# First stage of a four-layer graph kernel: sorted rows fetched early, loads and buffers rearranged

## Chip, cores, metric

One core of one Trainium2 chip. The time is the device time of one execution in microseconds (us). A kernel's executions agree within half a per cent. Each ratio is taken against the kernel before in the same rounds (its median was 2303.0 to 2304.5 in all of them). The changed kernel was timed in other rounds than the experiments, so differences from its median carry 1 to 2 us of noise. A difference from before is called a gain or a loss where the 95% interval of the ratio leaves out 1.

## The reference, cut

Four graph layers, each with a residual and a layernorm. Only the first, over a hypergraph, is concerned. B = 8 batches, N = 2048 nodes, E = 64 hyperedges, F = 64 features; H says which node belongs to which hyperedge (one certain and about 2 more per node).

```python
h = x @ W
s = leaky_relu(h @ a_node, 0.2)
alpha = softmax(where(H.T > 0, s[:, None, :], NEG), axis=-1)
agg = einsum('ben,bnf->bef', alpha, h)                       # hyperedge features
beta = sigmoid((h @ a_gn)[:, None, :] + (agg @ a_ge)[:, :, None])
all_he = elu(beta[..., None] * h[:, None] + (1 - beta[..., None]) * agg[:, :, None])
coefs1 = softmax(where(H[None] > 0, (tanh(elu(agg) @ fcW + fcb) @ av)[:, None, :], NEG), -1)
g = einsum('bne,benf->bnf', coefs1, all_he)                  # per node, over its hyperedges
industry = einsum('nm,bmf->bnf', adj / deg, x @ W_ind)       # 2048 x 2048 product
# ... attention over (industry, g), layernorm, three more layers that use adj
```

## The kernel before

The nodes are sorted by their number of hyperedges, so that a tile of 128 sorted nodes needs as many *slots* as its fullest node: 12 for tile 0, then 5, 5, 4, 4, 4, 3, ... , 1; 57 in all. The first stage has these parts:

- **x tiles** (16): h by TensorE, exponentials by ScalarE, three multiplies by VectorE, a write of the hidden rows to `hs_hbm`.
- **Adjacency load**: 32 halves of 512 KB through 4 staging buffers; ScalarE casts each into a tile that stays.
- **Tables** tab2, ts2 of the hyperedges, from the sums over all x tiles.
- **Sorted rows**: 16 gathers of H (hs), transposes, and a running count that gives `slot`.
- **Blocks**: per tile a gather `hrow` of sorted hidden rows; per slot three matmuls into a PSUM tile pz, then VectorE, ScalarE, VectorE, VectorE and GpSimd.
- **Filler**: 576 matmuls of the adjacency products (64 `du` for the degrees, 512 `u`), which a generator gives out between the slots to keep TensorE busy.

```python
for t in range(NT):                       # in the x stage's pool "pa"
    xt[t] = pa.tile([P, NP, P], F32, tag="xt", bufs=4)
    eng = nc.sync if t % 2 == 0 else nc.scalar
    eng.dma_start(xt[t], x_t[t])
# ... order, 16 x tiles, tables ...
for t in range(NT):                       # adjacency; staging also in "pa"
    for k in range(2):
        a = pa.tile([P, HN], F32, tag="a", bufs=4)
        eng = nc.sync if k == 0 else nc.scalar
        eng.dma_start(a, adj_t[t * P:(t + 1) * P, cols(k, HN)])
        nc.scalar.copy(adj[t][:, cols(k, HN)], a)
# ---- "pa" ends; pool "pb" takes its memory
filler = products()                       # du, then u; one matmul per next()
# ... hs: 16 gathers of h_ne by order; m2, pt, mt, pcm -> slot ...
def begin(t):
    # hrow <- gather of hs_hbm; split into hrh (ScalarE), hrl (VectorE);
    # o: one-hot per slot (GpSimd); ps = o @ ts2; R, rs, co (VectorE)
now = begin(0)
for t in range(NT):
    S, both, ohs, R, co = now
    for s in range(S):
        # pz = ident @ hrh + ident @ hrl + o[s] @ tab2
        if s == 0 and t + 1 < NT:
            fill(3)
            now = begin(t + 1)
        fill(10)
        # VectorE: z = pz * R; ScalarE: y = exp(z - 1); VectorE: y = min(max(z, 1), y)
        # VectorE: y * co; GpSimd: acc += y
```

Instructions of one engine run in the order that the build chose. The matmuls of blocks and filler keep the order of the program; everything else a scheduler orders, so the place of a loop in the program is a priority, not a time.

## Time and profile before

| | us |
|---|---|
| before, median of the 3 runs known at the prediction (spread) | 2305.34 (2302.71 to 2307.01) |
| first hrow gather, "the gate" | 131.68 |
| first pz * R multiply | 143.17 |
| next stage's first instruction | 343.14 |

How to read it: the kernel has 2301 us of trace, of which the first stage is 343. Most profile lines of before stand in the prediction. Here are, in addition, two of the waits of SyncE's queue and one of ScalarE (who waited, for what: us in total, times, longest), and the long stretch in one row of the view by stretches (bounds, length, busy TensorE, its weight loads, VectorE, ScalarE, GpSimd, granted clock, DMA share, GB/s):

```profile
SPq L364 <- DVE st L356: 25.5, 8, 7.7
SPq L238 <- PE ph L337: 21.7, 5, 5.6
```
```profile
ACT adj L437 <- DMA a<-in_adj_t: 26.5, 11, 6.3
```
```profile
143.20:330.40 187.20, 187.20 (x827) 152.44 (x827) 153.29 (x288) 51.73 (x88) 93.99 (x96) 0.97 0.23 70
```

The new queues are to cure the waits of the first fence. In the long stretch TensorE is busy for all of 187.2 us, and VectorE for 153.3.

### The profile page before, as it was taken

To read this page: it belongs to the slowest core of one execution; us is meant where nothing else is said; L and a number is where in the kernel's file an instruction comes from. 1 tells how busy PE (TensorE), PEld (TensorE's weight loads), DVE (VectorE), ACT (ScalarE), POOL (GpSimd) and SP (SyncE) were. 2 spreads that over 40 slices of the span, in tenths; PEclk is the share of its full clock that TensorE was granted. 3 is DMA by queue.
4 is the path that set the end of the run, shared out by engine and by line. 5 is a ranking of instruction groups with operands and counts; after the bars stand their busy time and mean duration, and the time that the engine had idled before them with its cause. 6 is when DMAs were issued, how large, how long until landed. Compare 5 with 4: busy or idle time off the path is not lost.

```text
span 2301.2 us, 19853 instructions
## 1 busy us (share of the span) xinstructions
PE 2009.9 (87%) x7382; PEld 1293.3 (56%) x7382; DVE 1119.7 (49%) x1895; ACT 361.7 (16%) x610; POOL 468.2 (20%) x432
## 2 busy tenths in 40 slices
PE   5379977887993999979999999999996999899994
PEld 3258863335882444447447446546543777777873
DVE  4347983554544122222882784685585334341322
ACT  2412323331111111101001001000000011111110
POOL 0155524550332332310010010011001001020202
PEclk8779998999995999989999999999998999999997
DMA  7712223220000000010000000000000223210000
GB/s 245 233 38 63 84 95 91 69 60 1 1 1 12 0 19 19 19 41 1 9 8 3 7 7 5 5 10 5 5 7 11 73 70 82 72 30 1 19 1 20
DMA packets 92586, 88.64 MB, mean 39 GB/s; under 512 B 62976, under 2 KB 63232, under 8 KB 92416
## 3 DMA queue, kind: packets, MB, share of 16 engines
q1 hardware_dynamic: 65072, 61.35, 9.3%
q10 hardware_dynamic: 23568, 16.95, 2.5%
q0 software_dynamic: 3840, 8.98, 1.5%
q8 instruction: 60, 0.98, 0.2%
q14 instruction: 46, 0.38, 0.1%
HBM read 66.22 MB, written 21.04 MB: 38 GB/s over the span
## 4 chain that ended last, share of the span: by engine, by line
PE 47%; DMA 8%; DVE 7%; POOL 3%; issue 2%; ACT 1%; SPq 0%; DVEq 0%; ACTq 0%; POOLq 0%
PE py L826 17%; PE u L773 10%; PE u L459 9%; PE u L171 8%; DMA a<-in_adj_t 7%; DVE a L932 2%; POOL ln_r L155 1%; PE pr L171 1%; PE tr L137 1%; DVE xg L115 1%; POOL r L838 1%; DVE ln_c L145 1%; DVE ln_v L151 1%; ACT r L149 0%; PE s L764 0%
## 5 line engine op out<-in xcount | busy, mean ns | idle before, releaser
L826 PE MATMUL py<-wp,xg 128*128 128x512 f32 x1024 | 448.6, 597 | 8.4 <-DVE pr L831 5.7
L826 PEld LDWEIGHTS py<-wp,xg 128*128 128x128 f32 x1024 | 193.6, 191 | 254.4 <-issue 216.3
L459 PE MATMUL u<-adj,vh 128*128 128x512 f32 x768 | 236.2, 410 | 24.7 <-ACT vh L166 20.9
L171 PE MATMUL u<-adj,hi 128*128 128x512 f32 x768 | 255.2, 413 | 0.0
L171 PE MATMUL u<-adj,lo 128*128 128x512 f32 x768 | 246.1, 400 | 1.0 <-DVE lo L897 1.0
L773 PE MATMUL u<-pt,xn 128*128 128x512 f32 x512 | 228.3, 604 | 8.3 <-DVE u L782 7.1
L459 PE MATMUL u<-adj,vl 128*128 128x512 f32 x768 | 228.9, 402 | 0.0
L831 DVE TENSOR_TENSOR pr<-py,emb_n 128x512 f32<-128x512 f32 x256 | 177.0, 691 | 51.9 <-PE py L826 37.4
L832 DVE TENSOR_REDUCE r<-pr 128x32 f32<-128x512 f32 x256 | 175.5, 685 | 8.1
L459 PEld LDWEIGHTS u<-adj,vh 128*128 128x128 f32 x768 | 141.8, 190 | 64.2 <-ACT vh L166 22.7
L773 PEld LDWEIGHTS u<-pt,xn 128*128 128x128 f32 x512 | 97.6, 193 | 130.6 <-issue 116.1
L171 PEld LDWEIGHTS u<-adj,hi 128*128 128x128 f32 x768 | 142.8, 190 | 41.0 <-issue 11.8
L171 PEld LDWEIGHTS u<-adj,lo 128*128 128x128 f32 x768 | 144.1, 189 | 34.5 <-DVE lo L897 1.4
L459 PEld LDWEIGHTS u<-adj,vl 128*128 128x128 f32 x768 | 141.4, 190 | 31.4 <-issue 0.7
L834 POOL TENSOR_TENSOR r<-r,bias 128x256 f32<-128x256 f32 x32 | 23.4, 730 | 636.4 <-DVE r L832 636.4
L155 POOL TENSOR_TENSOR ln_r<-ln_e,neg_half 128x8 f32<-128x8 f32 x64 | 105.7, 1651 | 185.5 <-DVE ln_e L153 185.2
L767 DVE TENSOR_SCALAR pt<-pt 128x512 f32<-128x512 f32 x64 | 48.8, 780 | 173.6 <-ACT pt L766 172.1
L771 POOL TENSOR_TENSOR acc<-acc,pt 128x512 f32<-128x512 f32 x60 | 79.6, 1327 | 163.3 <-DVE pt L767 160.5
L916 POOL TENSOR_TENSOR r<-r,xn 128x512 f32<-128x512 f32 x16 | 20.5, 1278 | 420.9 <-DVE r L915 420.9
L932 DVE SCALAR_TENSOR_TENSOR a<-a,adj 128x512 f32<-128x512 f32 x64 | 44.6, 697 | 124.7 <-DMA a<-in_adj_t 124.4
L156 DVE TENSOR_TENSOR xn<-ln_c,ln_r 128x512 f32<-128x512 f32 x48 | 41.8, 871 | 92.2 <-POOL ln_r L155 92.2
L655 POOL DMA_INDIRECT gn<-gs_hbm,rank x64 | 67.8, 1060 | 81.1 <-PE tr L137 62.3
(292 smaller groups left out, 2418.7 us busy)
## 6 DMA issues: line engine op xcount, KB each, us to landing
a<-in_adj_t SPq DMA_DIRECT2D x64, 256.0 KB, 2.8
a<-in_adj_t SPq DMA_DIRECT2D x16, 512.0 KB, 6.7
a<-in_adj_t ACTq DMA_DIRECT2D x16, 512.0 KB, 6.8
gs_hbm<-acc SPq DMA_DIRECT2D x16, 256.0 KB, 2.0
u_hbm<-ut SPq DMA_DIRECT2D x16, 256.0 KB, 2.8
ut<-u_hbm SPq DMA_DIRECT2D x16, 256.0 KB, 3.1
u_hbm<-u SPq DMA_DIRECT2D x16, 256.0 KB, 2.3
xg<-u_hbm SPq DMA_DIRECT2D x32, 128.0 KB, 2.7
```

The costliest lines, as they stand in the source:

```text
L155: nc.gpsimd.tensor_tensor(rstd, vare, neg_half[:, :groups], ALU.pow)
L156: nc.vector.tensor_tensor(dst, xc, rstd[:, :, None].to_broadcast([P, groups, F]), ALU.mult)
L171: tc.keep_in_program_order(nc.tensor.matmul(*args, **kw))
L459: nc.tensor.matmul(u[c], lhsT=half[:, j, :], rhs=adj[t][:, cols(c)], start=t == 0 and i == 0, stop=ends and not own,)
L655: nc.gpsimd.indirect_dma_start(out=gn[:, j, :], out_offset=None, in_=g_rows, in_offset=bass.IndirectOffsetOnAxis(ap=rank4[:, p, c * JT + j ...
L767: nc.vector.tensor_scalar(pt, pt, 1.0, None, op0=ALU.max)
L771: nc.gpsimd.tensor_tensor(acc, acc, pt, ALU.add)
L773: nc.tensor.matmul(u[p], lhsT=xn[:, p, t, :], rhs=pt, start=t == 0, stop=t == NT - 1)
L826: nc.tensor.matmul(py.rearrange("p o d -> p (o d)"), lhsT=xg[b][:, q, cols(j, P)], rhs=wp[:, q, cols(k)], start=q == 0, stop=q == 1,)
L831: nc.vector.tensor_tensor(pr, py, e_b, ALU.mult)
L832: nc.vector.tensor_reduce(r[:, j, b, cols(k, OH)], pr, AX.X, ALU.add)
L932: nc.vector.scalar_tensor_tensor(a, a, 1.0, adj[t][:, cols(k)].bitcast(F32), op0=ALU.mult, op1=ALU.not_equal, accum_out=left[:, t, k:k + 1],)
```

## The change

Its intent: do the sorted rows beside the loads rather than after them, so that the blocks begin earlier, and make room and queues for it. Cut to its core:

```diff
+    slot = hy.tile([P, N], BF16, name="slot")            # outer pool: live through the stage
+    hs = hy.tile([P, NT, E], F32, name="hs")
-            xt[t] = pa.tile(..., bufs=4)
-            eng = nc.sync if t % 2 == 0 else nc.scalar
-            eng.dma_start(xt[t], x_t[t])
+            xt[t] = pa.tile(..., bufs=6)
+            nc.scalar.dma_start(xt[t], x_t[t])
+        for t in range(NT):                               # adjacency loop, now ahead of the x tiles,
+            for k in range(2):                            # staging in a pool "ad" of its own
+                a = ad.tile([P, HN], F32, tag="a", name="a", bufs=4)
+                eng = nc.sync if k == 0 or t < NT // 2 else nc.scalar
+                eng.dma_start(a, adj_t[t * P:(t + 1) * P, cols(k, HN)])
+                nc.scalar.copy(adj[t][:, cols(k, HN)], a)
...
-            eng = nc.sync if t % 2 == 0 else nc.scalar
-            eng.dma_start(hs_hbm[t * P:(t + 1) * P, :], st)
+            nc.scalar.dma_start(hs_hbm[t * P:(t + 1) * P, :], st)
...   (the hs gathers, m2, pt, mt, pcm and slot move from the pool "pb" to behind the x tiles)
-            for c in range(NCH):                          # x for the products: 4 buffers -> 3,
-                fetch(0, c)                               # fetched and split within the du loop
+            for c in range(3):
+                fetch(0, c)
...
-                o = pl.tile([P, P], F32R, tag="o", name="o", bufs=17)
+                o = pl.tile([P, P], F32R, tag="o", name="o", bufs=13)
...
-                if s == 0 and t + 1 < NT:
-                    fill(3)
+                if s == max(0, S - 5) and t + 1 < NT:
+                    fill(3 if t else 0)
                     now = begin(t + 1)
-                fill(10)
+                fill(12 if t else 0)                      # no filler in tile 0, 12 per slot later
```

More of the change, by code (lines that the diff above doesn't have):

```diff
@@ L207, in tile_gnn_fast @@
     adj = [adj_pool.tile([P, N], F32R, name=f"adj{t}") for t in range(NT)]
-    with tc.tile_pool(name="pa", bufs=1) as pa, tc.tile_pool(name="pa_ps", bufs=1, space=PSUM) as pps:
+    with tc.tile_pool(name="ad", bufs=1, side="right") as ad, tc.tile_pool(
+        name="pa", bufs=1
+    ) as pa, tc.tile_pool(name="pa_ps", bufs=1, space=PSUM) as pps:
         m_n = pa.tile([P, NT, E], F32, name="m_n")
@@ L235, in tile_gnn_fast @@
         for t in range(NT):
-            xt[t] = pa.tile([P, NP, P], F32, tag="xt", name=f"xt{t}", bufs=4)
-            eng = nc.sync if t % 2 == 0 else nc.scalar
-            eng.dma_start(xt[t], x_t[t])
+            xt[t] = pa.tile([P, NP, P], F32, tag="xt", name=f"xt{t}", bufs=6)
+            nc.scalar.dma_start(xt[t], x_t[t])
+        HN = N // 2
+        for t in range(NT):
[4 more added lines that the diff above has]
+                nc.scalar.copy(adj[t][:, cols(k, HN)], a)
         pw = pps.tile([P, 2], F32, tag="sm", name="pw", bufs=2)
@@ L372, in tile_gnn_fast @@
         )
+        for t in range(NT):
+            nc.gpsimd.indirect_dma_start(
+                out=hs[:, t, :], out_offset=None, in_=h_ne,
+                in_offset=bass.IndirectOffsetOnAxis(ap=order[:, t:t + 1], axis=0),
+            )
+        for c in range(NCH):
+            m2 = pa.tile([P, JT, 2, E], F32, tag="m2", name="m2", bufs=2)
+            for i in range(2):
+                nc.vector.tensor_scalar(m2[:, :, i, :], hs[:, c * JT:(c + 1) * JT, :], 0.0, None, op0=ALU.is_gt)
+            pt = pps.tile([P, C], F32, tag="sm", name="pt", bufs=2)
+            for j in range(JT):
+                nc.tensor.transpose(pt[:, cols(j, P)], m2[:, j].rearrange("p i e -> p (i e)"), ident)
+            mt = pa.tile([P, C], BF16, tag="mt", name="mt", bufs=2)
+            nc.scalar.copy(mt, pt)
+            pcm = pps.tile([P, C], F32, tag="sm", name="pcm", bufs=2)
+            nc.tensor.matmul(pcm, lhsT=tri2, rhs=mt, start=True, stop=True)
+            nc.vector.tensor_tensor(slot[:, cols(c)], pcm, mt, ALU.mult)
         gv = pagg[:, :, 0:G * (F + 1)].rearrange("p k (g c) -> p k g c", c=F + 1)
@@ L428, in tile_gnn_fast @@
         nc.vector.tensor_tensor(ts2[E:P, :], tsf, ts2[0:E, :], ALU.subtract)
-        HN = N // 2
-        for t in range(NT):
-            for k in range(2):
-                a = pa.tile([P, HN], F32, tag="a", name="a", bufs=4)
-                eng = nc.sync if k == 0 else nc.scalar
-                eng.dma_start(a, adj_t[t * P:(t + 1) * P, cols(k, HN)])
-                nc.scalar.copy(adj[t][:, cols(k, HN)], a)
     def load_x(dst, p, c):
@@ L472, in tile_gnn_fast @@
     with ExitStack() as pb_scope:
-        pb = pb_scope.enter_context(tc.tile_pool(name="pb", bufs=1))
+        pb = pb_scope.enter_context(tc.tile_pool(name="pb", bufs=1, side="right"))
         pps = pb_scope.enter_context(tc.tile_pool(name="pb_ps", bufs=1, space=PSUM))
@@ L482, in fetch @@
             def fetch(p, c):
-                xc[p, c] = pb.tile([P, JT, P], F32, tag="x", name="xc", bufs=4)
+                xc[p, c] = pb.tile([P, JT, P], F32, tag="x", name="xc", bufs=3)
                 load_x(xc[p, c], p, c)
@@ L489, in parts @@
                 part[c] = split(pb, xc.pop((p, c)), f"v{c}", 1, [P, JT, P])
-            for c in range(NCH):
+            for c in range(3):
                 fetch(0, c)
             for t in range(NT):
+                if t in (2, 3, 4):
+                    parts(0, t - 2)
+                    if t == 2:
+                        fetch(0, 3)
+                if t == 8:
+                    parts(0, 3)
                 for c in range(NCH):
@@ L496, in products @@
                     yield
-            for c in range(NCH):
-                parts(0, c)
             for c in range(NCH):
@@ L514, in products @@
                         if p + 1 < NP and t % JT == JT - 1:
-                            if g == 0:
+                            if g == 0 and t // JT < 3:
                                 fetch(p + 1, t // JT)
-                            else:
+                            elif g == 1:
                                 parts(p + 1, t // JT)
+                                if t // JT == 0:
+                                    fetch(p + 1, 3)
                         if p == 0 and g == 0 and t == 3:
@@ L547, in fill @@
                 next(filler, None)
-        slot = pb.tile([P, N], BF16, name="slot")
-        with tc.tile_pool(name="pc", bufs=1) as pc:
-            hs = pc.tile([P, NT, E], F32, name="hs")
-            for t in range(NT):
-                nc.gpsimd.indirect_dma_start(
-                    out=hs[:, t, :], out_offset=None, in_=h_ne,
-                    in_offset=bass.IndirectOffsetOnAxis(ap=order[:, t:t + 1], axis=0),
-                )
-            for c in range(NCH):
-                m2 = pc.tile([P, JT, 2, E], F32, tag="m2", name="m2", bufs=2)
-                for i in range(2):
-                    nc.vector.tensor_scalar(m2[:, :, i, :], hs[:, c * JT:(c + 1) * JT, :], 0.0, None, op0=ALU.is_gt)
-                pt = pps.tile([P, C], F32, tag="mm", name="pt", bufs=3)
-                for j in range(JT):
-                    transpose(pt[:, cols(j, P)], m2[:, j].rearrange("p i e -> p (i e)"))
-                mt = pc.tile([P, C], BF16, tag="mt", name="mt", bufs=2)
-                nc.scalar.copy(mt, pt)
-                pcm = pps.tile([P, C], F32, tag="mm", name="pcm", bufs=3)
-                mm(pcm, lhsT=tri2, rhs=mt, start=True, stop=True)
-                nc.vector.tensor_tensor(slot[:, cols(c)], pcm, mt, ALU.mult)
         pl = pb_scope.enter_context(tc.tile_pool(name="pl", bufs=1))
```

## The prediction

> **What bounds the kernel now.** I began with the chain of waits. It covers only 719.9 to 2301.2 us, stages that the diff does not touch, so it says nothing about the first stage. I therefore read that stage in stretches: busy us of each engine, granted clock, share of the 16 DMA engines, GB/s.
>
> ```profile
> 10.00:20.00 10.00, 5.41 (x31) 4.20 (x28) 6.43 (x33) 3.65 (x7) 0.00 (x0) 0.98 0.94 338
> ...
> 70.00:80.00 10.00, 5.86 (x30) 3.67 (x31) 6.31 (x18) 5.11 (x12) 0.00 (x0) 1.00 0.88 279
> ...
> 90.00:105.00 15.00, 2.71 (x18) 1.86 (x16) 0.66 (x4) 8.22 (x12) 0.00 (x0) 0.50 0.59 187
> 105.00:131.60 26.60, 6.78 (x20) 3.40 (x20) 7.16 (x16) 5.10 (x9) 15.33 (x16) 0.50 0.43 100
> 131.60:142.90 11.30, 6.18 (x15) 4.48 (x16) 2.35 (x7) 0.62 (x1) 10.12 (x18) 0.50 0.17 47
> 142.90:165.10 22.20, 22.20 (x87) 18.05 (x86) 13.81 (x25) 5.10 (x9) 11.69 (x14) 0.86 0.09 25
> ...
> 260.00:300.00 40.00, 40.00 (x180) 32.48 (x179) 37.14 (x69) 11.33 (x19) 19.26 (x20) 1.00 0.21 70
> ...
> 330.40:343.10 12.70, 2.66 (x11) 1.54 (x10) 10.16 (x21) 2.39 (x4) 2.52 (x2) 0.76 0.28 104
> ```
>
> The first number after the comma is TensorE. Up to 105 us the transfers bound the stage (0.6 to 0.94 of the DMA engines); from 105 to 142.9 TensorE does 13 us of work in 38; from 142.9 to 330.4 it is never idle; the last 12.7 us belong to VectorE. The timeline and the waits name the edges:
>
> ```profile
> 78.81 0.68 DVE L360 TENSOR_TENSOR ex<-ph,ex 128x512 f32<-128x512 f32 x1
> ...
> 94.55 0.17 DVE L428 TENSOR_TENSOR ts<-tsm,ts 64x16 fp32r<-64x16 f32 x1 [1.05 <-ACT ts L427]
> ...
> 131.68 0.94 POOL L575 DMA_INDIRECT hrow<-hs_hbm,order  x1 [5.56 <-DVE slot L568]
> ...
> 142.93 1.05 PE L171 MATMUL du<-adj,ones_r 128*128 128x512 f32 x2
> 143.17 0.70 DVE L616 TENSOR_TENSOR pz<-pz,R 128x512 f32<-128x512 f32 x1 [0.61 <-PE pz L171]
> ...
> 343.14 0.17 DVE L120 MEMSET bd_ind<- 128x128 f32 x1 [2.47 <-DMA gs_hbm<-acc]
> ```
> ```profile
> POOL hs L553 <- ACT adj L437: 103.4, 1, 103.4
> ```
>
> The last of the 16 x tiles is done at 79.5; the hyperedge tables at 94.7; the gathers of sorted rows (hs) begin only when the last adjacency cast has freed memory, near 105.4; their transposes and slot tables end at 131.4; the first block's gather follows at 131.7, its first multiply at 143.2; the next stage starts at 343.1.
>
> **What the Trainium skill says.** "DMA: Bandwidth & Descriptors", section "Issuing engines are not separate DMA queues": transfers from different engines end up on the same 16 DMA engines, and several issuers save only issue time. The trace agrees: a 512 KB adjacency half lands in 6.7 us from SyncE and 6.8 from ScalarE. So "x on its own queue" buys no bandwidth, only freedom from blocking. The same page, "Anatomy of one DMA", says that any wait for a semaphore happens on the issuing sequencer before dispatch. The trace agrees: SyncE's queue waits 25.5 us in total for VectorE's st and 21.7 us for TensorE's ph, with adjacency loads queued behind. The other side: a transfer issued by ScalarE holds up ScalarE's arithmetic. "TensorE: Matmul & The Clock Gate", "What's actually happening": the idle default is half clock, and sustained work releases it. The trace agrees: 0.50 from 90 to 142.9, 1.00 later.
>
> **The change part by part.**
>
> 1. Removed: the stretch from 105.4 to 131.7, 26.3 us of gathers, transposes and slot tables. The same 16 gathers, 16 transposes and 4 slot multiplies now lie beside the loads.
>
> 2. Moved: the gate. In the built program the first hrow gather waits for the last hs_hbm write and for the last VectorE instruction of the first pool (ts2), because the block pool reuses its memory. It no longer waits for an adjacency cast directly. So everything hangs on when the x tiles end, 79.5 in the old kernel.
>
> 3. The x tiles get later. In the built order ScalarE casts 5 adjacency halves, then tiles 0 and 1, 6 more casts, tiles 2 and 3, further casts up to the 17th, tile 4, casts up to the 29th, tile 5; tiles 6 to 15 come only after the 32nd cast. VectorE's tiles 2 and 3 also stand behind the compares of gathered rows. Estimates from the old durations: the order table is ready near 23 (25.9 before; two x tiles' vector work of 3 us moves behind it, about 1 us is lost to later small loads). Gathers go out every 1.25 us and land in some 3 us; the eighth lands near 37 and holds ScalarE at cast 11 for about 6 us, the twelfth near 42 holds it about 4 us more. By cast 17, about 50 us. The other 15 halves are 7.9 MB; at 280 to 310 GB/s that is 25 to 28 us, so the casts end near 78. Total bytes to then: 16.8 MB adjacency, 3.4 x, 0.5 + 0.5 H, 1.3 hs writes = 22.5 MB; at the 320 to 340 GB/s of the full stretches that alone is 68 us after a start at 7, which agrees. Tiles 6 to 15 then need TensorE's 1.09 + 1.17 us each, with little slack: about 2.35 us x 10 = 23.5. The last tile ends near **101.5**, 22 us later than now.
>
> 4. The tables take 15.2 us now (79.5 to 94.7); without adjacency casts between them on ScalarE about 12. The gate opens near 113.5, against 131.7: **18 us earned**. The setup of a first block stays 11.3 to 11.5 us.
>
> 5. Tile 0 has 12 slots and no filler now. The first du matmul stands behind the 13th pz, and pz has 3 buffers, so it waits for about 10 slots on VectorE: 10 x 3 x 0.69 = 20.7, plus tile 1's small operations and split, 1.3 + 0.7, plus leading pz multiplies: **about 24 us** in which TensorE has only 3 matmuls per slot. In the old kernel du began with the first slot. So du begins at 113.5 + 11.5 + 24 = 149, against 142.9: 6 us *later*.
>
> 6. Given back: of the 57 slots the old stretch from du to the last filler holds 53 (one before it, three after), the new one 44 (13 before it), so it loses 9 x 3 = 27 pz matmuls: 27 x 0.2325 (two in 0.465 at full clock) = 6.3 us. 188 becomes 181.5. The filler (12 per slot) now lasts to the last slot, so the tail from last filler matmul to the next stage shrinks from 12.7 to about 5.5 (two ut multiplies 1.3, a write 2.8, the last slot's chain).
>
> Sum: 149 + 181.5 + 5.5 = 336 against 343.1: **7 us saved**, all else unchanged. 2305.3 - 7 = **2298 us**. Of the 26 us removed most is lost to the later x tiles (22), and the rest to tile 0 without filler; what remains comes from the balance of the tail.
>
> **The rivals.**
>
> A. The whole stretch is earned. If the x tiles kept their 79.5, the gate would open near 92, and the sum gives 29 us saved, 2276 us. For it: the diff means it so, and x has six buffers and its own queue. Against it: ScalarE's order, ten tiles behind the last cast.
>
> B. The load becomes the bound. The adjacency now has at most four halves in flight, mostly from one queue, and ScalarE stalls twice in front of casts. At 230 GB/s, which the old stretch 40 to 50 shows, 22.5 MB takes 98 us and the casts end near 105; the x tiles end near 128 and the kernel loses about 20 us: 2325. Against it: 338 GB/s where nothing blocked, 10 to 20 us.
>
> C. VectorE becomes the bound in the long stretch. It is at 37.1 of 40 us from 260 to 300. But there it is beside 10 filler per slot; 12 filler leave 45 slots' multiplies for the same filler. I estimate 142 us of VectorE in 181. Then nothing changes there; if its order nevertheless holds TensorE, a few us are lost, near 2302.
>
> D. Later stages shift by layout or clock: I see no mechanism, and allow 3 us.
>
> **Range and chances.** The x tiles' end is uncertain by about 7 us, tile 0 by 3, tail and later stages by 3 each: together some 9 us, so 8 in 10 lie within about 13: 2284 to 2311. Two per cent is 46 us. Even rival A saves less; the whole idle time before du is what would be needed. Faster 0.02, same 0.965, slower 0.015.
>
> **What would show it right or wrong.** The last ex multiply of the x tiles near 101 (79.5 before), with casts ended near 78 and x tiles alone after them. The first hrow gather near 113, released by ts2. Twelve pz triples with no du among them and VectorE near full for 24 us. The first du near 149, TensorE never idle from there for about 181 us, and the last filler within 6 us of the next stage, which begins near 336. It is wrong if the x tiles end before 90 (rival A) or after 110 (B), if du begins before 135, or if TensorE shows gaps in the long stretch (C).

## The result, and the profile after

| | before (with a fourth run) | after |
|---|---|---|
| median, us (runs) | 2304.53 (4) | 2305.65 (4) |
| spread | 2302.71 to 2307.01 | 2302.95 to 2309.39 |
| profiled execution, clock | 2301.2, 0.944 | 2302.0, 0.943 |

The ratio is 1.0005 with a 95% interval of 0.9986 to 1.0024: no difference. Ratios here are the mean time of one kernel's fast runs over that of the other's of the same rounds, so not quite the ratio of the medians quoted.

The first stage in the changed kernel, by stretches (columns as above):

```profile
20.00:50.00 30.00, 16.54 (x67) 10.62 (x67) 10.88 (x38) 15.13 (x23) 15.43 (x16) 0.60 0.90 317
50.00:88.00 38.00, 6.24 (x24) 4.04 (x25) 3.78 (x12) 16.24 (x21) 0.00 (x0) 0.64 0.66 228
88.00:111.30 23.30, 21.31 (x112) 13.65 (x112) 18.27 (x52) 5.17 (x23) 0.00 (x0) 0.93 0.39 137
111.30:123.10 11.80, 5.75 (x28) 3.94 (x28) 5.43 (x14) 3.12 (x8) 0.03 (x1) 0.70 0.06 23
```
```profile
134.60:161.90 27.30, 16.77 (x42) 10.31 (x42) 26.26 (x41) 8.13 (x14) 18.83 (x22) 0.63 0.11 29
161.90:338.00 176.10, 176.03 (x797) 144.12 (x795) 136.13 (x268) 46.75 (x79) 80.05 (x78) 0.99 0.26 79
338.00:341.70 3.70, 0.00 (x0) 0.00 (x0) 2.36 (x5) 0.00 (x0) 0.00 (x0) 0.94 0.71 263
```

To 50 us the transfers run at 317 GB/s. Then for 38 us everything is slow: DMA engines at 0.66, ScalarE busy 16 of 38, VectorE nearly idle. Only at 88 do the remaining ten x tiles run, at TensorE's pace (21.31 of 23.30 us). Tile 0 (second fence) has VectorE at 26.3 of 27.3 us and TensorE at 16.8, at a granted clock of 0.63; from 161.9 TensorE is never idle. The timeline names the edges (start, length, engine, line, operation, idle time before it and what ended that):

```profile
49.74 0.49 ACTq L248 DMA_DIRECT2D a<-in_adj_t  x1
49.77 1.04 ACT L249 CAST adj<-a 128x1024 fp32r<-128x1024 f32 x1
50.28 0.49 ACTq L248 DMA_DIRECT2D a<-in_adj_t  x1
...
57.77 1.99 ACT L249 CAST adj<-a 128x1024 fp32r<-128x1024 f32 x2 [6.59 <-DMA a<-in_adj_t]
...
110.50 0.68 DVE L371 TENSOR_TENSOR ex<-ph,ex 128x512 f32<-128x512 f32 x1
...
123.07 0.94 POOL L580 DMA_INDIRECT hrow<-hs_hbm,order  x1 [79.34 <-DVE ts L457]
...
134.58 0.70 DVE L622 TENSOR_TENSOR pz<-pz,R 128x512 f32<-128x512 f32 x1 [0.53 <-PE pz L171]
...
161.89 1.48 PE L171 MATMUL du<-adj,ones_r 128*128 128x512 f32 x3
...
341.66 0.17 DVE L120 MEMSET bd_ind<- 128x128 f32 x1 [1.31 <-DMA u_hbm<-ut]
```

ScalarE issues two adjacency halves at 49.74 and 50.28; the next cast in its stream needs one of them, and begins 7.5 us later. This occurs four times (with idle times of 6.6, 3.9 in two pieces, 4.4 and 5.5 us), since eight of the halves are ScalarE's. The gate opens at 123.07, released by ts2, 8.6 us earlier than before; but the stretch from the first multiply (134.58) to the next stage (341.66) is 207.1 us, 7.1 longer than before. The two cancel to 1.5 us. Of that, little reaches the next stage's own first gather (343.72 before, 343.44 after), and the rest of the kernel is as it was within the spread of the runs.

So the question is twofold: why the gate opens no earlier, and why the stretch behind it got longer.

### The profile page after: what moved, and what is told of

Read it like the earlier page. It is cut to its first block, busy times and chain, and to the rows that moved or that the text cites. A ratio compares the mean times of both kernels' runs of the same rounds, so it can differ in the third digit from the quotient of the medians.

```text
span 2302.0 us, 19820 instructions
## 1 busy us (share of the span) xinstructions
PE 2010.0 (87%) x7382; PEld 1295.4 (56%) x7382; DVE 1118.9 (49%) x1895; ACT 363.1 (16%) x610; POOL 470.0 (20%) x432
## 4 chain that ended last, share of the span: by engine, by line
PE 47%; DMA 8%; DVE 7%; POOL 3%; issue 2%; ACT 1%; SPq 0%; DVEq 0%; ACTq 0%; POOLq 0%
PE py L832 17%; PE u L779 10%; PE u L479 9%; PE u L171 8%; DMA a<-in_adj_t 7%; DVE a L938 2%; POOL ln_r L155 1%; PE pr L171 1%; PE tr L137 1%; DVE xg L115 1%; POOL r L844 1%; DVE ln_c L145 1%; DVE ln_v L151 1%; ACT r L149 0%; PE s L770 0%
## 5 line engine op out<-in xcount | busy, mean ns | idle before, releaser
L171 PEld LDWEIGHTS u<-adj,hi 128*128 128x128 f32 x768 | 143.6, 191 | 40.9 <-issue 11.5
```

Of the source, the lines that this page charges most:

```text
L171: tc.keep_in_program_order(nc.tensor.matmul(*args, **kw))
```

## The experiments

Theory: (a) the halves that ScalarE issues itself lay their landing time bare and hold everything behind the casts; (b) without filler in tile 0 TensorE stands idle there, and its work is done later. Rivals: the transfers are at their rate anyway; VectorE's chain sets the length of the stretch whatever the filler does. Twelve kernels ran, all gave correct results. Edits are against the changed kernel unless "before" is said. The table at the end of this section collects gates and stretches.

**1. All adjacency loads on SyncE.**

```diff
-                eng = nc.sync if k == 0 or t < NT // 2 else nc.scalar
+                eng = nc.sync
```

> The changed kernel with all 32 adjacency halves issued by SyncE (the changed kernel gives 8 of them to ScalarE). Theory 1: those halves stand in ScalarE's own stream just before the casts that need them, so their landing time of 6.5 to 8 us is laid bare four times; then the casts end near 78 instead of 88, the first block gather opens near 113.5 instead of 123.1, and the kernel takes about 2296 us, 9 less than the changed one. Rival 2: the transfers are at their rate anyway, or the other waits (sorted rows, buffers) hold the casts: the casts end within 2 us of 88 and the time stays within 3 us of 2305.

Measured: 2290.85 us, ratio to before 0.9939 (0.9925 to 0.9952). The casts end at 79.2, the last x tile at 96.4, the gate opens at 108.3:

```profile
108.29 0.95 POOL L580 DMA_INDIRECT hrow<-hs_hbm,order  x1 [66.16 <-DVE ts L457]
```

ScalarE's waits for adjacency transfers up to 90 us, first in the changed kernel, then here, and the stretch 60 to 80 of both in the same order:

```profile
ACT adj L249 <- DMA a<-in_adj_t: 26.3, 14, 6.6
```
```profile
ACT adj L249 <- DMA a<-in_adj_t: 13.2, 17, 1.7
```
```profile
60.00:80.00 20.00, 0.00 (x0) 0.00 (x0) 0.48 (x2) 9.93 (x12) 0.00 (x0) 0.50 0.77 261
```
```profile
60.00:80.00 20.00, 9.90 (x42) 6.47 (x39) 6.75 (x19) 13.30 (x21) 0.00 (x0) 0.79 0.90 347
```

The longest wait falls from 6.6 to 1.7 us, and in the same 20 us 347 instead of 261 GB/s move, x tiles now among them. Theory (a) holds for the casts, which end 8.8 us earlier. The gate gains more than expected, 14.8 us, for a reason that the edit does not show: the build put ScalarE's work in another order too. Behind the last cast come seven x tiles here and ten in the changed kernel, so the last one ends 17.2 us after the casts and not 23.2. These 6.0 us and the 8.8 make up the 14.8; no run separates them. Of the 14.8 us 12.7 reach the next stage (341.66 to 328.97), since the stretch is 2.1 us longer.

**2. Filler in tile 0 as everywhere.**

```diff
-                    fill(3 if t else 0)
+                    fill(3)
-                fill(12 if t else 0)
+                fill(12)
```

> The changed kernel with filler matmuls in tile 0 as in all other tiles (12 per slot, 3 before the next block). Theory 1: TensorE's work from the gate on is fixed (about 747 matmuls of 0.2325 us) and tile 0 without filler leaves about 11 us of it undone; then du begins near 136 instead of 161.9, the next stage near 331 instead of 341.7, and the kernel takes about 2294 us. Rival 2: VectorE carries tile 0, and filler before its pz only delays it, so what TensorE gains at the start VectorE lacks at the end: 2300 to 2306 us, with the tail from last filler to next stage over 10 us.

Measured: 2305.4 us, 1.0007 (0.9993 to 1.002): nothing. Theory (b) in this form fell. du begins at 135.8 and TensorE is full up to 313, and there the filler is used up:

```profile
300.00:313.00 13.00, 13.00 (x59) 10.65 (x58) 9.11 (x19) 3.00 (x5) 5.75 (x6) 1.00 0.14 44
313.00:340.00 27.00, 17.12 (x46) 10.50 (x44) 26.83 (x58) 7.90 (x14) 9.62 (x9) 0.61 0.27 88
```

Before 313 TensorE is full and VectorE is at 0.70; after it VectorE is full (26.83 of 27.00) and TensorE is not. The stretch with VectorE as the bound has only moved from the start to the end.

**3. x tiles first: the adjacency loop told after the tables**, as in the kernel before, the rest of the change kept.

```diff
-        (adjacency loop ahead of pw, rank and x tiles)
         nc.vector.tensor_tensor(ts2[E:P, :], tsf, ts2[0:E, :], ALU.subtract)
+        (adjacency loop, same text, still with staging in "ad")
```

> The changed kernel with the adjacency loop told to the scheduler after the hyperedge tables, as in the kernel before, all else of the change kept (staging memory of its own, sorted rows early, x on ScalarE's queue, no filler in tile 0). Theory 1: only the order on ScalarE made the x tiles late; then the last x tile ends near 78, the first block gather goes out near 92 to 95 (before: 131.7, changed: 123.1), du begins near 132, the next stage near 312, and the kernel takes about 2272 us. Rival 2: x tiles and loads share ScalarE's queue, and the loads of x that now wait there for buffers push casts and tiles alike: the gate stays after 115 and the time over 2295 us.

Measured: 2288.49 us, 0.9932 (0.9919 to 0.9946). The last x tile ends at 83.9 and the gate opens at 100.25, but the first multiply comes only at 119.83, where SyncE alone had brought it too. Timeline:

```profile
100.25 0.94 POOL L581 DMA_INDIRECT hrow<-hs_hbm,order  x1 [51.78 <-DVE ts L449]
...
114.16 2.94 ACT L457 CAST adj<-a 128x1024 fp32r<-128x1024 f32 x3 [3.86 <-DMA a<-in_adj_t]
...
117.85 0.79 PE L171 MATMUL pz<-hrh,ident_r 128*128 128x512 f32 x1 [9.17 <-ACT hrh L166]
```

The order did keep the x tiles late, as theory 1 says; but a new wait took the place of the old. The block's own cast hrh stands behind the last adjacency casts in ScalarE's stream, and the last three wait for a half that ScalarE issued. Half of the expected gain came.

**4. The kernel before with the 64 du matmuls ahead of the sorted rows.**

```diff
+        fill(64)
         slot = pb.tile([P, N], BF16, name="slot")
```

> The kernel before with one line added: the 64 du matmuls are given out ahead of the gathers of sorted rows, so that they run in the stretch 105 to 132 in which TensorE idles. Nothing else of the change. Theory 1: the end of the stage is set by TensorE's work left when the long stretch begins; 64 x 0.2325 = 14.9 us of it leave, the next stage begins near 330 instead of 343 and the kernel takes about 2291 us. Rival 2: VectorE (37 of 40 us busy from 260 to 300) takes over as the bound, or the slot tables come later because their transposes stand behind du: 2300 to 2310 us.

Measured: 2302.56 us, 0.9991 (0.9977 to 1.0005): nothing. du ran early, from 95.1 on, and TensorE had 15 us less to do, but with 10 filler per slot the last filler matmul came at 312 rather than 330, and from there to 341.9 VectorE carried the stage alone, busy for 25.96 of the last 29.2 us. The gate also opened 3.6 us later (135.3). So both parts of rival 2 came, the first by the same mechanism as in run 2.

**5. The kernel before with one part of the change: sorted rows early** (hs and slot in the outer pool, gathers and count behind the x tiles; nothing else).

```diff
+    slot = hy.tile([P, N], BF16, name="slot")
+    hs = hy.tile([P, NT, E], F32, name="hs")
+        (hs gathers, m2, pt, mt, pcm, slot behind the x tiles, as in the change)
-        (the same in pool "pc" ahead of the blocks)
```

> The kernel before with one part of the change alone: sorted rows fetched, transposed and counted in the x stage (hs and slot in the outer pool); queues, buffers, order of the adjacency loop and filler as before. Theory 1: the stretch of 26 us is simply removed, and the first block gather goes out when the last adjacency cast frees the memory, near 106; first multiply near 118, next stage near 317, kernel about 2279 us. Rival 2: the compares and casts of the sorted rows stand in the order of VectorE and ScalarE and hold up x tiles and casts as in the changed kernel; the gate opens after 115 and the time is over 2288 us.

Measured: 2286.16 us, 0.9921 (0.9906 to 0.9937), between the two expectations. The gate is at 115.73, after the last cast, as theory 1 has it, but the casts end at 115 instead of 105:

```profile
115.73 0.94 POOL L575 DMA_INDIRECT hrow<-hs_hbm,order  x1 [69.60 <-ACT adj L458]
```

Of 26 us removed, 16 are earned at the gate, and all of them at the end: the stretch behind is 199.8 us, as before (200.0). This one part is faster than the whole change, so that the other parts together give its gain back. Most of the casts' delay is there by the 17th of them (78.2 against 70.6); what causes it was not tested.

**6. The changed kernel with an even filler: 9 per slot in all tiles.**

```diff
-                    fill(3 if t else 0)
+                    fill(3)
-                fill(12 if t else 0)
+                fill(9)
```

> The changed kernel with filler spread evenly: 9 per slot in every tile, tile 0 too (the changed one gives 0 in tile 0 and 12 later; with 12 everywhere the filler ran out at 313.6 and VectorE needed until 345.8). Theory 1: TensorE and VectorE are both close to full, and only an uneven spread makes each wait for the other in turn; TensorE needs about 747 matmuls x 0.25 = 187 us from 136, so the last filler is near 323, the next stage near 328, the kernel about 2290 us. Rival 2: from the first multiply to the next stage VectorE's chain takes its 200 to 207 us whatever the filler (143.2 to 343.1, 134.6 to 341.7, 136.0 to 345.8 in the runs so far): 2300 to 2306 us.

Measured: 2285.43 us, 0.9918 (0.9903 to 0.9933). The gate is even some 3 us later than in the changed kernel (125.9), yet the next stage begins at 327.4:

```profile
327.37 0.17 DVE L120 MEMSET bd_ind<- 128x128 f32 x1 [2.71 <-DMA u_hbm<-ut]
```
```profile
137.40:323.00 185.60, 185.23 (x836) 151.38 (x836) 162.93 (x309) 53.84 (x93) 104.08 (x100) 0.98 0.27 80
```

TensorE is full and VectorE at 0.88 over one and the same 186 us. Theory 1 holds. Beside run 2 this tells the two apart: the same filler, from the same slot on, at 12 per slot gains nothing and at 9 per slot 20 us.

**7. Both repairs and du in the setup**: SyncE loads; 48 du matmuls ahead of the first block; 8 filler per slot.

```diff
+        fill(48)
         now = begin(0)
-                fill(12 if t else 0)
+                fill(8)
```

> The changed kernel with all adjacency loads on SyncE, 48 of the 64 du matmuls given out ahead of the first block's setup, and 8 filler per slot in every tile. Theory 1: gate near 108, du runs in the setup and delays the first multiply from 119.8 to about 127; then 700 matmuls x 0.25 = 175 us, next stage near 307, kernel about 2269 us. Rival 2: VectorE's chain takes 200 us from the first multiply: next stage near 327 to 333, 2288 to 2295 us.

Measured: 2264.07 us, 0.9832 (0.9818 to 0.9845), near theory 1: the 48 du run from 105.8 to 118.7, beginning ahead of the gate (107.3), the first multiply comes at 123.0 and the next stage at 303.9.

**8. x tiles first, SyncE loads, 9 filler.** (Edits of runs 1, 3 and 6 together.)

> The changed kernel with the adjacency loop told after the tables (x tiles first), all its loads on SyncE, and 9 filler per slot in every tile. Theory 1: without loads in ScalarE's stream the casts end near 95 instead of 117 and no longer hold the first block; first multiply near 110, next stage near 302, kernel about 2263 us. Rival 2: the casts wait for ScalarE's place in the order behind x tiles and end after 110 all the same; first multiply near 118, next stage near 310 if the even filler works, 2272 us, and near 325, 2286 us, if it does not.

Measured: 2262.89 us, 0.9814 (0.9802 to 0.9826). The gate opens at 97.6, the casts end at 106 rather than at the 95 of theory 1, and the block's cast hrh still stands right behind them (106.07). That costs only about 1 us now: from the gate to the first multiply (110.0) it is 12.4 us, against 11.5 in the kernels before and after and 19.6 in run 3. The next stage begins at 299.6. The time of theory 1 came, though one of its steps was wrong.

**9. Run 4 with thinner filler (kernel before).**

```diff
+        fill(64)
         slot = pb.tile([P, N], BF16, name="slot")
-                fill(10)
+                fill(8)
```

> The kernel before with the 64 du matmuls given out ahead of the sorted rows (as in the run that gained nothing, where the filler then ran out at 312 and VectorE went on alone to 342) and the filler thinned from 10 to 8 per slot, so that it lasts to the end. Theory 1 (both engines are near full, an uneven spread costs): about 683 matmuls x 0.25 = 171 us from 146.8, last filler near 318, next stage near 325, kernel about 2286 us. Rival 2 (du early delays the block, and VectorE's chain keeps its 195 us): 2298 to 2303 us.

Measured: 2289.17 us, 0.9941 (0.9923 to 0.9959). du ahead of the rows gained nothing at 10 per slot and gains 14 us at 8, with the gate at the same place (134.4 and 135.3). This shows on the old kernel what run 6 shows on the new one.

**10. The best of all: x tiles first, SyncE loads, 48 du in the setup, 8 filler.** (Edits of runs 1, 3 and 7.)

> The best so far (x tiles first, all adjacency loads on SyncE) with 48 du matmuls ahead of the first block's setup and 8 filler per slot. Theory 1: the gate stays near 97.6, du fills the setup, the first multiply comes near 113 instead of 110, and the stretch from there to the next stage is 181 us as in the other run with du in the setup: next stage near 294, kernel about 2257 us. Rival 2: VectorE, at 38 of 40 us, is the floor: its 190 us from the first multiply stay, next stage near 303, 2266 us.

Measured: 2257.43 us, 0.98 (0.9785 to 0.9815). Faster than before (2303.00 in these rounds) and after by 46 and 48 us. What is left is two engines close to full in one stretch:

```profile
113.00:291.00 178.00, 174.79 (x787) 141.73 (x787) 161.20 (x307) 53.35 (x93) 100.54 (x100) 0.98 0.28 85
```

**11. The kernel before with the queue part alone**: all x tiles on ScalarE with 6 buffers, all writes of hidden rows on ScalarE.

```diff
-            eng = nc.sync if t % 2 == 0 else nc.scalar
-            eng.dma_start(xt[t], x_t[t])
+            nc.scalar.dma_start(xt[t], x_t[t])        # and bufs=6; the same for hs_hbm
```

> The kernel before with the queue part alone: all x tiles on ScalarE's queue with 6 buffers, all writes of hidden rows on ScalarE. Theory 1: the sum of bytes is the same and the gate hangs on the last adjacency cast and the 26 us behind it: x tiles may end some us earlier or later, the casts end within 4 us of 105, the kernel takes 2299 to 2308 us. Rival 2: SyncE's queue, which waits 25.5 us for VectorE and 21.7 us for TensorE in the kernel before, is freed for adjacency loads: casts end near 95 and the kernel takes about 2293 us.

Measured: 2308.83 us, 1.002 (1.0005 to 1.0034): about 5 us slower. The x tiles end 12 us earlier, the casts 3 us later, and the gate follows the casts and the sorted rows:

```profile
66.87 0.68 DVE L359 TENSOR_TENSOR ex<-ph,ex 128x512 f32<-128x512 f32 x1
```
```profile
135.52 0.94 POOL L573 DMA_INDIRECT hrow<-hs_hbm,order  x1 [5.41 <-DVE slot L566]
```

**12. The two repairs and nothing else**: edits of runs 1 and 6.

> The changed kernel with both repairs and nothing else: all adjacency loads on SyncE, and 9 filler per slot in every tile. Theory 1: the two causes are independent, one sets the gate (108.3 with SyncE alone), the other the stretch behind it (190.0 from first multiply to next stage with 9 filler); first multiply near 119.8, next stage near 310, kernel about 2270 us (2305.65 less 14.8 and 20.2). Rival 2: they overlap, the earlier gate brings VectorE's floor forward: the stretch stays over 196 us, 2276 us or more.

Measured: 2270.87 us, 0.9857 (0.984 to 0.9873), against 2270 expected. The two causes add up: the gate opens 15.6 us earlier than in the changed kernel and the stretch is 17.3 us shorter, where run 1 alone had 14.8 and run 6 alone 17.1.

All runs together, in us; the stretch is from the first multiply to the next stage:

| kernel | median | gate | first multiply | next stage | stretch |
|---|---|---|---|---|---|
| before (10 per slot) | 2304.53 | 131.7 | 143.2 | 343.1 | 200.0 |
| after (0, then 12) | 2305.65 | 123.1 | 134.6 | 341.7 | 207.1 |
| 1 SyncE loads | 2290.85 | 108.3 | 119.8 | 329.0 | 209.2 |
| 2 12 in all tiles | 2305.40 | 124.5 | 136.0 | 345.8 | 209.8 |
| 3 x first | 2288.49 | 100.3 | 119.8 | 328.0 | 208.2 |
| 4 before, du early | 2302.56 | 135.3 | 146.8 | 341.9 | 195.1 |
| 5 before, rows early | 2286.16 | 115.7 | 127.2 | 327.0 | 199.8 |
| 6 9 in all tiles | 2285.43 | 125.9 | 137.4 | 327.4 | 190.0 |
| 7 SyncE, du in setup, 8 | 2264.07 | 107.3 | 123.0 | 303.9 | 180.8 |
| 8 x first, SyncE, 9 | 2262.89 | 97.6 | 110.0 | 299.6 | 189.6 |
| 9 before, du early, 8 | 2289.17 | 134.4 | 145.9 | 327.6 | 181.7 |
| 10 x first, SyncE, du in setup, 8 | 2257.43 | 96.7 | 113.0 | 295.5 | 182.5 |
| 11 before, x queue | 2308.83 | 135.5 | 147.0 | 346.4 | 199.4 |
| 12 SyncE, 9 | 2270.87 | 107.5 | 118.9 | 308.7 | 189.8 |

The last column goes by the filler pattern and hardly by the gate: 207 to 210 with 12 per slot (with or without tile 0), 199 to 200 with 10 (195 with du taken out beforehand), 190 with 9, 181 to 183 with 48 or 64 du taken out beforehand and 8 per slot. The fewer buffers for o and x and the later place of `begin` were not tested alone. But run 9, which has none of them, has the stretch of runs 7 and 10 within 1 us.

## Why the prediction was right, and where it was off

That the time stays the same was predicted, and so was its main reason: what the removed stretch earns is lost to later x tiles and to a tile 0 without filler. The small gain of 7 us did not come: the next stage begins only 1.5 us earlier than before, and the medians differ by 1.1 us the other way, within the noise. Step by step:

| term of the sum | predicted | measured |
|---|---|---|
| casts end (step 3) | 78 | 88.0 |
| last x tile (step 3) | 101.5 | 111.2 |
| gate (step 4) | 113.5 | 123.1 |
| setup of a first block | 11.3 to 11.5 | 11.5 |
| tile 0, to the first du (step 5) | 24 | 27.3 |
| du to the last filler (step 6) | 181.5 | 176.0 |
| tail to the next stage | 5.5 | 3.7 |
| next stage | 336 | 341.7 |

The errors of the x tiles (9.7 us) and of tile 0 (3.3) made the stage longer, those of the long stretch (5.5) and of the tail (1.8) shorter. That they partly cancelled, so that the sum was off by 5.7 only, is luck.

- **Steps 1 and 2 were right.** The sorted rows lie beside the loads and the gate waits for ts2. That the 26 us are worth only 16 at the gate by themselves (run 5) shows that even beside the loads the rows cost something.
- **Step 3 is where the size failed**, in the rate for the last 15 halves: "at 280 to 310 GB/s that is 25 to 28 us". They took 38, from 50 to 88, with 228 GB/s moving in all. I had noted that "a transfer issued by ScalarE holds up ScalarE's arithmetic", but did not apply it to the eight halves that ScalarE issues just ahead of the casts that need them. Run 1 takes this away: from the 17th cast at 50.4 to the end of the last at 79.2 it needs 28.8 us, so that my figure holds for a kernel in which the loads are not in ScalarE's stream. Rival B named such stalls, and its 230 GB/s is near the measured rate, but by chance: it was taken from another stretch and for all the bytes. The rest of the step was right: ten x tiles at 2.35 us, 23.5 predicted and 23.3 measured.
- **Step 4** passed the 10 us on; the tables themselves took 11.0 us against 12.
- **Step 5** was right in kind, 3.3 us short in size. VectorE is full and its multiplies of pz take their 0.69 us, but nine y x co multiplies took 1.00 on average and not 0.69, which is 2.8 us; the split hrl took 1.56 and not the 0.7 reckoned. The Trainium skill, "SBUF — State Buffer", section "Who interferes with whom", says that a VectorE instruction with two inputs in SBUF contends with a GpSimd instruction that reads SBUF, while one with a single SBUF input, outside the modes in which it uses two ports, does not. The trace agrees: here a GpSimd accumulation is under way when a pz multiply (pz lies in PSUM) and then a y x co multiply start; the first takes its 0.69, the second 1.26,

```profile
140.65 0.69 DVE L622 TENSOR_TENSOR pz<-pz,R 128x512 f32<-128x512 f32 x1
140.68 1.28 POOL L632 TENSOR_TENSOR acc<-acc,y 128x512 f32<-128x512 f32 x1
141.25 1.26 DVE L631 TENSOR_TENSOR y<-y,co 128x512 f32<-128x512 f32 x1
```

  Of the nine, the six that start during an accumulation take 0.81 to 1.65 us, and the three that meet none 0.68 to 0.69. No run tests this by itself.
- **Step 6** reckoned with 6.3 us less (188 less 6.3 is 181.7, not 181.5), and the trace shows 11.6 (187.7 to 176.0). The number of matmuls was right: between the first du and the last filler 132 of pz are left of 160, which is 28 x 0.2325 = 6.5 us. Most of the rest goes with the granted clock: in the old stretch it was 0.55 from 142.9 to 150 and 0.77 from 165 to 180, in the new one 0.71 from 161.9 to 165 and 0.98 from 180 to 260, and 1.00 otherwise. An estimate from these: 6.6 us of full-clock time were missing in the old stretch and 2.5 in the new, 4.1 us of difference. Why the clock fell in these places was not tested.
- **The rivals.** A did not occur, because of ScalarE's order as argued; run 3 shows that with the other order the x tiles end at 83.9. C was set aside rightly for the changed kernel, where VectorE is at 0.77 of the long stretch, but it does occur in this stage: in runs 2 and 4 VectorE is what ends it. D: the later stages did not shift beyond the spread.

Where the gain of 26 us went, then: 17.7 of it never reached the gate, and of these 14.8 come back with the loads on SyncE and the order that the build then chose (run 1); of the 8.6 that did reach it, 7.1 were given back in the stretch behind it, whose work was cut into a part for VectorE alone (27.3 us) and a part for TensorE alone. Runs 1, 6 and 12 show both causes and their sum.

The Trainium skill, "Perfetto Trace Analysis", section "Optimization Strategy", says that a kernel can have several regimes with different most-contended engines, and that interleaving the regimes may help. The runs agree: with the same work, two regimes one after the other took 209.8 us (run 2), interleaved 190.0 (run 6).

## What to carry to other kernels

Filler that keeps one engine busy should last as long as the work of the other engine: count both, and divide. Here, handing it out too fast (12 per slot from the start, a stretch of 209.8 us) cost as much as handing out none in tile 0 and 12 later (207.1). A load that a computing engine issues just ahead of its own use of the data lays its landing time bare, here up to 6.6 us at a time; try an engine that has no such work in its stream. After a change to one engine's work, look at the order that the build then chose: in run 1 it made 6.0 of 14.8 us. And test the parts of a change singly: here one part alone gained 17 us, which the others together gave back.

## What the Trainium skill lacked or had wrong

- "DMA: Bandwidth & Descriptors", section "Issuing engines are not separate DMA queues", says that the issuing engine matters only for the time to initiate a transfer, which is small. It lacks the effect of place: with eight of 32 loads issued by ScalarE, each ahead of the cast that needs it, the last cast ended at 88.0 us, and with the same loads from SyncE at 79.2.
- No page gives a measure for how fast filler is to be handed out. Here 12, 10 (in the kernel before) and 9 filler matmuls per slot made 210, 200 and 190 us of the same work; the best of these rates lies near the filler over the slots, (576 - 45)/57 = 9.3, where 45 are given out with the 15 later blocks.
